# The last expert blocks of a stage return their results by a product with ones

## The chip, the cores and the metric

The kernel runs on one core of one Trainium2 chip. The metric is the device time of one execution in microseconds; before the change its median over three runs is 806.35 us (805.9 to 808.5).

## The reference, cut to what matters

Four batches of 256 tokens with 128 features go through four layers. Each layer adds a gated attention and a gated feed-forward to x. Two of the four feed-forwards route tokens to experts, and the change touches only these:

```python
# layer 1: one of 8 experts for each token
scores = feats @ centroids.T
expert = jnp.argmax(scores, axis=1)
onehot = jax.nn.one_hot(expert, E)
alpha = sigmoid(sum(feats * centroids[expert]))
ys = vmap(_sublayer, ...)(feats, gamma, beta, W1, b1, W2, b2)   # normed -> 128x512 -> relu -> 512x128
y = jnp.einsum('te,etd->td', onehot, ys)
out = alpha * y + (1.0 - alpha) * feats
# layer 3: two of 8 experts for each token, and a shared one
scores = softmax(xt @ gate_w.T)
topk_w, topk_i = jax.lax.top_k(scores, 2)
eo = einsum(silu(xt @ gate_k) * (xt @ up_k), down_k)            # for each expert
y = weighted sum of the two experts' eo;  shared = silu(xt @ sh_gate) * (xt @ sh_up) @ sh_down
# in the model
x = x + tanh(g_ffn[l]) * ffn_l(layernorm(x))
```

The reference computes every expert for every token. The kernel computes only the chosen ones.

## The kernel before, in words

**Groups and streams.** The batches are taken in two groups of two (G = 2), 512 tokens in a group, four tiles of 128 tokens. `chain(g)` writes one group's work in order: attention and feed-forward of layer 0, attention 1, `route1` and `feed1` (layer 1's experts), attention 2 and feed-forward 2, attention 3, `route3` and `feed3` (layer 3's experts). Each piece is a Python generator, a stream. A stream yields an estimate in us of what it has just written, and `run_streams` always continues the stream with the smallest sum. So the order of instructions on each engine is fixed when the kernel is built; the two groups and their pieces interleave by these estimates. On the chip each engine works its queue strictly in this order, and an instruction that waits holds up everything behind it on its engine. SP's queue issues most loads, ACT's queue some loads, the outputs and the writes of expert results, POOL's queue all indirect transfers.

**Slots and blocks.** `Routed.assign` counts the tokens of each expert and gives every choice of a token a slot (`si`, one number for each token tile and choice) in a list where each expert's slots begin at a multiple of 128. A block is 128 slots and has one expert. With 512 choices there are 11 blocks (layer 1), with 1024 there are 15 (layer 3); slots that no token holds carry zeros. `dispatch` (L744) scatters the tokens' rows to their slots in memory, one indirect transfer of 128 rows for each token tile and choice, from POOL; `empty_slots` (L662) has zeroed that memory from SP near the beginning. `fetch` (L770) reads four blocks of rows back with one transfer on SP.

**A stage's call.** `Routed.run` goes over the blocks. For block j: `ask` reads the expert's number into a register of SP and loads the down weights (L801), and starts the next fetch; `before` copies the up weights on DVE (L808) and transposes the block on PE (L810; the result is scaled or copied at L1109 or L1318 on DVE); `up` is the first product and its activation (L1115 to L1121, or L1324 and L1283, L1284); `down` is the second (L819, four matmuls, recorded as eight), its result is copied by ACT (L824) to a tile `ys` of four blocks, and each full `ys` is written to memory (`back`, L826). `down` of a block stands on PE behind `up` of the next.

**Results.** When all blocks are done, `run` gathers from `back` the row of each token's slot (L851): four indirect transfers in layer 1, eight in layer 3, on POOL. `feed1` adds them to the experts' bias, weighs them by alpha and adds the result to x (L1125 to L1131); `feed3` adds them to the shared expert's result with their weights (L1338), multiplies by the gate into x (L1344) and writes the output (L1348).

The steps that follow: after `feed1`, the next attention of that group begins with statistics of x (L270, L272 on DVE, L274 and L276 on POOL), query transposes (L1165), scores (L328), row maxima (L338); `finish2` normalises x again (`x2f`, L282). Tiles `feat`, 20 in rotation, hold most intermediate results, `ys` and the gathered rows among them.

Names in the profile: `x1n`, `x3f` are the rows that are scattered, `rows_f` the slots' memory, `xs_f` the fetched rows, `pt_f` and `xT_f` their transpose, `ph_f` or `pp_f` the first product, `h_f` its activation, `wd_f` the down weights, `py_f` the second product, `ys_f` its copy, `back_f` the results' memory, `yg_f` the gathered rows.

Of the kernel before, what the change touches and what calls it, by code (L numbers as in the profile page):

```python
# [18 lines left out]
P = 128  # L19
B, S, D = 4, 256, 128  # L20
T = S // P
G = 2
# [14 lines left out]
def flamingo_kernel(ctx: ExitStack, tc: tile.TileContext, a: dict, out: bass.AP):  # L37
# [619 lines left out]

    def empty_slots():
        for layer, k in ((1, 1), (3, 2)):
            for g in range(B // G):  # L660
                t = dram.tile([blocks(k) * BLOCK, D], F32, tag=f"rows{layer}", name=f"rows_f{layer}_{g}")
# [6 lines left out]
    class Routed:  # L668
# [7 lines left out]
        def assign(self, hots, src, after=()):  # L676
# [62 lines left out]
            yield from self.dispatch()  # L739

        def dispatch(self):

            for i, t, src in self.moves:
# [12 lines left out]
                yield 1.3  # L756

# [25 lines left out]
        def run(self, width, weights, down_weights, turn, up, cost):  # L783
# [4 lines left out]
            name, n = self.name, self.n  # L788
            back = dram.tile([n * BLOCK, D], F32, tag=f"back{len(self.slots)}", name=f"back_{name}")
            bv = back.rearrange("(j p) d -> p j d", p=P)  # L790
# [24 lines left out]
            def down(j, h):  # L815
# [9 lines left out]
                if j % 4 == 3 or j == n - 1:  # L825
                    nc.scalar.dma_start(out=bv[:, j // 4 * 4 : j + 1, :], in_=ys[0][:, 0 : j % 4 + 1, :])  # L826

# [7 lines left out]
            for j in range(n):  # L835
                st, xT = ready.pop(0)
                h = up(st, xT, f"{name}_{j}")
                if behind:
                    down(*behind)
                ask(j + 2)  # L840
                behind = (j, h)
                if j + 2 < n:
                    ready.append(before(j + 2))
                yield cost
            down(*behind)
            yield 4.0
            self.out = []
            for i, si in enumerate(self.slots):
                y = feat(f"yg_{name}_{i}").rearrange("p (t d) -> p t d", t=GT)
                for t in range(GT):  # L850
                    nc.gpsimd.indirect_dma_start(  # L851
                        y[:, t, :], None, back, bass.IndirectOffsetOnAxis(ap=si[:, t : t + 1], axis=0)
                    )
                self.out.append(y)
            yield 8.0
# [219 lines left out]
    def route1(g):  # L1075
# [22 lines left out]
        acc = work.tile([P, GT, D], F32, tag="acc", name=f"f1acc_{g}")  # L1098
        nc.vector.tensor_copy(acc, pb)
        groups1[g] = (r, fe, al, acc)  # L1100
        r.fetch(0)
        yield 4.0


    def feed1(g):
        r, fe, al, acc = groups1[g]
# [17 lines left out]
        yield from r.run(518, shared["we1"], a["L1f_down"], turn, up, 1.9)  # L1124
# [382 lines left out]
```

## Time and profile before

| what | us |
|---|---|
| median of three runs | 806.35 |
| the profiled execution | 805.46 |
| its span, first to last instruction | 803.7 |
| PE busy (matmuls) | 719.7 |
| DVE busy | 462.6 |
| ACT busy | 314.9 |
| POOL busy | 133.5 |
| the 24 gathers of results (L851), mean of one | 0.994 |
| the 24 scatters of rows (L744), all | 25.3 |

The profiled execution is the profiler's record of one run: its own time is 1.8 us more than its span. Engines are PE (matmuls; PEld are its weight loads), DVE, ACT, POOL and SP. Issuing a transfer is not counted as busy, except on POOL, where building an indirect transfer is an instruction of about 1 us. An entry in square brackets says how long the engine had been idle before the instruction and what ended that. The granted clock is that of PE, as a share of full speed; its mean over the execution is 0.958.

### The profile page before, as it was taken

Reading aid. Unit: us, or ns where it says so; the run is one execution under the profiler, and the core shown is the slowest. Engines: PE = TensorE matmul, PEld = TensorE weight load, DVE = VectorE, ACT = ScalarE, POOL = GpSimd, SP = SyncE. Lnnn points to the kernel's source line nnn. Section 1 sums busy time; section 2 is a strip of 40 time slices with the busy share of each in tenths; the row PEclk is TensorE's granted clock in tenths of the full one; section 3 lists DMA queues with packets and bytes.
Section 4 is the critical chain, followed back from the end, with each engine's and each line's share of the span. In section 5 each row is a group of like instructions: output and inputs, shape, how many; then the busy total and the mean of one; then the engine's idle time right before and its main releaser. Section 6 shows DMA issues by size and latency. Waiting matters only on the chain.

```text
span 803.7 us, 14819 instructions
## 1 busy us (share of the span) xinstructions
PE 719.7 (90%) x5756; PEld 515.6 (64%) x5756; DVE 462.6 (58%) x1179; ACT 314.9 (39%) x609; POOL 133.5 (17%) x233
## 2 busy tenths in 40 slices
PE   5989998999999998997897899979999988799990
PEld 4556676766666665597864456546666645599990
DVE  3475573556577587775767476553454436665461
ACT  2536555343444423232453445435542442322330
POOL 3010121321110001313212131010000004040043
PEclk9899999999999999999997899999999989999995
DMA  6820101101023002354471000000100200435631
GB/s 202 239 61 2 54 2 53 54 1 54 1 76 110 2 8 53 97 199 150 135 261 39 1 28 2 1 1 1 53 8 1 60 1 24 148 89 146 164 106 49
DMA packets 52986, 54.98 MB, mean 68 GB/s; under 512 B 7274, under 2 KB 40084, under 8 KB 52660
## 3 DMA queue, kind: packets, MB, share of 16 engines
q1 hardware_dynamic: 41252, 44.07, 18.5%
q10 hardware_dynamic: 10128, 6.82, 2.8%
q0 software_dynamic: 1536, 3.15, 1.3%
q8 instruction: 45, 0.74, 0.4%
q14 instruction: 25, 0.20, 0.1%
HBM read 44.52 MB, written 9.50 MB: 67 GB/s over the span
## 4 chain that ended last, share of the span: by engine, by line
PE 70%; DVE 15%; issue 6%; ACT 4%; POOL 2%; DMA 2%; DVEq 0%; POOLq 0%; ACTq 0%; SPq 0%
PE po_a L486 7%; PE sc_a L472 7%; PE pp_f L1324 6%; DVE nmx L338 4%; PE py_f L819 4%; PE po_a L374 4%; PE ps_a L501 4%; PE sc_a L328 4%; PE pf_a L559 3%; PE st_a L355 3%; PE pw_qh_a L444 3%; PE pv_a L458 3%; PE pw_kh_a L444 3%; PE f0pp L987 2%; PE pb_a L526 2%
## 5 line engine op out<-in xcount | busy, mean ns | idle before, releaser
L338 DVE TENSOR_REDUCE nmx<-sc_a 128x2 f32<-128x512 f32 x128 | 79.4, 683 | 27.1 <-PE sc_a L328 27.1
L366 ACT ACTIVATE pw_a<-st_a 128x512 f32<-128x512 f32 x128 | 66.1, 605 | 36.7 <-PE st_a L355 36.6
L472 PE MATMUL sc_a<-qh_a,kh_a 64*128 64x256 f32 x512 | 69.8, 402 | 0.6 <-DVE kh_a L72 0.4
L1042 ACT ACTIVATE pr_a<-pr_a 128x1024 f32<-128x1024 f32 x32 | 33.8, 1057 | 91.7 <-DVE pr_a L1041 85.4
L486 PE MATMUL po_a<-pr_a,va_a 128*64 128x256 f32 x512 | 63.3, 392 | 1.1 <-ACT va_a L76 0.6
L472 PEld LDWEIGHTS sc_a<-qh_a,kh_a 64*128 64x128 f32 x512 | 46.5, 190 | 23.1 <-issue 10.3
L1324 PE MATMUL pp_f<-xT_f,st_f 128*128 128x128 f32 x480 | 58.7, 276 | 1.9 <-DVE xT_f L1318 1.9
L819 PE MATMUL py_f<-wd_f,h_f 128*128 128x128 f32 x416 | 56.7, 279 | 1.7 <-DVE h_f L1121 1.7
L1324 PEld LDWEIGHTS pp_f<-xT_f,st_f 128*128 128x128 f32 x480 | 56.1, 192 | 3.3 <-issue 2.6
L819 PEld LDWEIGHTS py_f<-wd_f,h_f 128*128 128x128 f32 x416 | 51.8, 195 | 2.8 <-DVE h_f L1121 2.1
L486 PEld LDWEIGHTS po_a<-pr_a,va_a 128*64 128x64 f32 x512 | 35.2, 139 | 24.4 <-issue 5.6
L1215 DVE TENSOR_SCALAR pr_a<-pr_a 128x1024 f32<-128x1024 f32 x32 | 22.1, 691 | 47.7 <-ACT pr_a L1214 47.7
L1038 DVE SCALAR_TENSOR_TENSOR pr_a<-maskT,sc_a 128x512 f32<-128x512 uint8 x64 | 40.9, 680 | 11.7 <-PE sc_a L472 11.6
L1214 ACT ACTIVATE pr_a<-sc_a 128x512 f32<-128x512 f32 x64 | 34.0, 604 | 33.0 <-PE sc_a L472 33.0
L328 PE MATMUL sc_a<-kp,qp 32*128 32x256 f32 x512 | 44.2, 429 | 0.3 <-DVE lT L1223 0.3
L355 PE MATMUL st_a<-qm_a,kp 32*128 32x256 f32 x512 | 40.8, 428 | 2.4 <-DVE qm_a L348 2.4
L374 PE MATMUL po_a<-pw_a,va_a 128*32 128x256 f32 x512 | 42.5, 412 | 0.0
L494 ACT COPY oT_a<-po_a 128x512 f32<-128x512 f32 x32 | 18.6, 586 | 50.2 <-PE po_a L486 48.7
L355 PEld LDWEIGHTS st_a<-qm_a,kp 32*128 32x128 f32 x512 | 26.0, 200 | 17.7 <-DVE nmx L338 7.0
L1284 DVE TENSOR_TENSOR h_f<-pp_f,sl_f 128x512 f32<-128x512 f32 x30 | 20.6, 688 | 25.4 <-PE pp_f L1324 15.9
L851 POOL DMA_INDIRECT yg_f<-back_f,si_f x24 | 23.9, 994 | 67.8 <-DMA back_f<-ys_f 42.0
L991 POOL TENSOR_TENSOR wide<-f0wb,wide 128x512 f32<-128x512 f32 x16 | 20.3, 1270 | 88.9 <-DVE wide L990 80.4
(337 smaller groups left out, 1329.6 us busy)
## 6 DMA issues: line engine op xcount, KB each, us to landing
wd_f<-in_L3f_down_dram SPq DMA_DIRECT2D x30, 256.0 KB, 3.2
wd_f<-in_L1f_down_dram SPq DMA_DIRECT2D x22, 256.0 KB, 4.0
f0wb<-f0wd SPq DMA_DIRECT2D x32, 128.0 KB, 3.2
rb_a<-rw_a SPq DMA_DIRECT2D x16, 256.0 KB, 3.8
we<-in_L3f_experts_dram SPq DMA_DIRECT2D x8, 512.0 KB, 9.1
xs_f<-rows_f SPq DMA_DIRECT2D x10, 256.0 KB, 3.6
back_f<-ys_f ACTq DMA_DIRECT2D x10, 256.0 KB, 5.7
we<-in_L1f_experts_dram SPq DMA_DIRECT2D x8, 259.0 KB, 5.4
```

Source lines behind the costliest of these rows:

```text
L328: nc.tensor.matmul(self.sc[j][:, qt, :], lhsT=self.qp[c // 2][r, c % 2, qt * P : (qt + 1) * P], rhs=self.kp[c // 2][r, c % 2, :], start=Tr ...
L338: nc.vector.tensor_reduce(self.nmx[c % 2][:, :, j, 8], self.sc[j], AX.X, ALU.max, negate=True)
L355: nc.tensor.matmul(st[j][:, kt, :], lhsT=self.kp[c // 2][r, c % 2, kt * P : (kt + 1) * P], rhs=self.qm[c // 2][r, c % 2, :], start=True, s ...
L366: nc.scalar.activation(pw[:, i], st[2 * n + i], AF.Exp, scale=SCALE8)
L374: nc.tensor.matmul(po[r, :], lhsT=self.va[:, kt, 4 * c + j, :], rhs=pw[j // 2][:, j % 2, kt, :], start=(kt == 0), stop=(kt == T - 1),)
L444: nc.tensor.matmul(pp[:, ci, :], lhsT=w[:, c * P : (c + 1) * P], rhs=src, start=True, stop=True)
L472: nc.tensor.matmul(sc[jj][:, kt * S : (kt + 1) * S], lhsT=self.kh[c // 2][r, c % 2, kt * P : (kt + 1) * P], rhs=self.qh[c // 2][r, c % 2, ...
L486: nc.tensor.matmul(po[64 * jj : 64 * jj + 64, ci, :], lhsT=self.va[cp // 2][:, kt, 4 * (cp % 2) + 2 * ci + jj, :], rhs=self.prs[2 * cp + c ...
L819: nc.tensor.matmul(py, lhsT=h[:, f, :], rhs=wd[:, f * P : (f + 1) * P], start=(f == 0), stop=(f == 3))
L1038: nc.vector.scalar_tensor_tensor(pr[:, jj, :], maskT[:, b].rearrange("p t q -> p (t q)"), -1e32, sc[jj], ALU.mult, ALU.add)
L1214: nc.scalar.activation(pr[:, jj, :], sc[jj], AF.Exp)
L1324: nc.tensor.matmul(pp[i][:, f * P : (f + 1) * P], lhsT=st[:, 512 * i + f * P : 512 * i + (f + 1) * P], rhs=xT, start=True, stop=True,)
```

## The change

A table names three of the four calls and how many of their last blocks are concerned: the last 3 of 11 in layer 1, both groups, and the last 4 of 15 in layer 3's second group. Layer 3's first group has none.

- For these calls, `empty_slots` also zeroes the last blocks of `back` and a small list `tags`, one number (layer 1) or two (layer 3) for each slot.
- After `dispatch`, a new stream `label` scatters to each slot its token's number in the group (from 1) and, in layer 3, its weight: four indirect transfers on POOL in layer 1, eight in layer 3. Then SP reads the last blocks' tags to a tile, and that read waits for all of these scatters.
- `belongs` makes on DVE, for each of the last blocks, a matrix of 128 slots by 512 tokens that is one (or the weight) where the slot is the token's; a count of 1 to 512 for this comes from POOL.
- `sent_back` multiplies this matrix with the block's results in `ys` on PE: four matmuls, one for each token tile. All last blocks add up in one tile of PSUM, `pb_f`.
- The last blocks are not written to `back`. The gathers form a stream of their own, which begins when the other blocks have been written; rows of slots in the last blocks read as zero. Their adds on DVE stand in that stream.
- Bias, alpha and gate are now applied piece by piece and everything is added to x directly: features and bias in `route1`, the shared expert in `shared3`, gathered rows and the product as they come. The tile `acc` and the final multiplies are gone. In layer 3 the output of a batch is issued after the last add to it.

The diff, cut to its core:

```diff
+    LAST = {"f1_0": 3, "f1_1": 3, "f3_1": 4}
+    results_of = {}
     def empty_slots():
...
+                if last:
+                    nc.sync.dma_start(out=bv[:, n - last :, :], in_=zero.unsqueeze(1).to_broadcast([P, last, D]))
+                    tags = dram.tile([n * BLOCK, k], F32, tag=f"tags{layer}", name=f"tags_f{layer}_{g}")
+                    cleared = nc.sync.dma_start(
+                        out=tags.rearrange("(p j) k -> p (j k)", p=P), in_=zero[:, 0 : n * k]
+                    )
...
             yield from self.dispatch()
+            self.last = LAST.get(name, 0)
+            if self.last:
+                self.labelled = Stream(self.label(weights))
...
+        def label(self, weights):
+            tags, cleared = results_of[self.name][2]
+            k, last = len(self.slots), self.last
+            src = small.tile([P, k, GT, k], F32, tag=f"tag{k}", name=f"tag_{self.name}", bufs=1)
+            nc.gpsimd.iota(src[:, :, :, 0], pattern=[[0, k], [P, GT]], base=1, channel_multiplier=1, ...)
+            if weights:
+                for i, w in enumerate(weights):
+                    nc.gpsimd.tensor_copy(src[:, i, :, 1], w)
+            yield 1.0
+            writes = []
+            for i, si in enumerate(self.slots):
+                for t in range(GT):
+                    write = nc.gpsimd.indirect_dma_start(
+                        tags, bass.IndirectOffsetOnAxis(ap=si[:, t : t + 1], axis=0), src[:, i, t, :], None
+                    )
...
+                    nc.gpsimd.memset(spare, 0.0)
+                    yield 1.3
+            self.tags = small.tile([P, last, k], F32, tag=f"tags{k}", name=f"tags_{self.name}", bufs=1)
+            read = nc.sync.dma_start(
+                out=self.tags, in_=tags.rearrange("(j p) k -> p j k", p=P)[:, self.n - last :, :]
+            )
+            for w in writes:
+                self.need(read, w)
...
-                if j % 4 == 3 or j == n - 1:
+                if j >= n - last:
+                    back_to.append((j, ys[0][:, j % 4, :]))
+                elif j % 4 == 3 or j == n - 1 - last:
                     nc.scalar.dma_start(out=bv[:, j // 4 * 4 : j + 1, :], in_=ys[0][:, 0 : j % 4 + 1, :])
+                    if j == n - 1 - last:
+                        back_to.append(Stream(gathered(), 4.0))
+            def gathered():
+                out = []
+                for i, si in enumerate(self.slots):
+                    y = feat(f"yg_{name}_{i}").rearrange("p (t d) -> p t d", t=GT)
+                    for t in range(GT):
+                        nc.gpsimd.indirect_dma_start(
+                            y[:, t, :], None, back, bass.IndirectOffsetOnAxis(ap=si[:, t : t + 1], axis=0)
+                        )
+                        yield 1.3
+                    out.append(y)
+                yield 1.5
+                for i, y in enumerate(out):
+                    for t in range(GT):
+                        add(i, t, y[:, t, :])
+                        yield 0.5
+            def belongs(j):
+                if "count" not in once:
+                    once["count"] = feat(f"count_{name}")
+                    nc.gpsimd.iota(once["count"], pattern=[[1, GN]], base=1, channel_multiplier=0, ...)
+                m = feat(f"m_{name}_{j}")
+                tag = self.tags[:, j - (n - last), :]
+                if len(self.slots) == 2:
+                    nc.vector.tensor_scalar(m, once["count"], tag[:, 0:1], tag[:, 1:2], ALU.is_equal, ALU.mult)
+                else:
+                    nc.vector.tensor_scalar(m, once["count"], tag[:, 0:1], None, ALU.is_equal)
+                return m
+            def sent_back(j, y):
+                if "sums" not in once:
+                    once["sums"] = ps_mm([P, GT, D], f"pb_{name}")
+                for t in range(GT):
+                    nc.tensor.matmul(once["sums"][:, t, :], lhsT=ms[j][:, t * P : (t + 1) * P], rhs=y,
+                                     start=(j == n - last and t == 0), stop=(j == n - 1 and t == GT - 1))
...
             for j in range(n):
                 st, xT = ready.pop(0)
                 h = up(st, xT, f"{name}_{j}")
+                if len(back_to) > 1:
+                    sent_back(*back_to.pop())
                 if behind:
                     down(*behind)
+                if j == n - 1 - last and last:
+                    yield from joined(self.labelled)
+                if j >= n - last:
+                    ms[j] = belongs(j)
                 ask(j + 2)
...
+            if len(back_to) > 1:
+                sent_back(*back_to.pop())
             down(*behind)
-            yield 4.0
...
-            yield 8.0
+            yield HOP
+            if last:
+                sent_back(*back_to.pop())
+            yield from joined(*back_to)
+            if last:
+                for t in range(GT):
+                    add(None, t, once["sums"][:, t, :])
...
     def feed1(g):
+        def add(i, t, y):
+            xt = x[G * g + t // T][:, t % T, :]
+            nc.vector.scalar_tensor_tensor(xt, y, al[:, t : t + 1], xt, ALU.mult, ALU.add)
...
     def feed3(g):
+        def add(i, t, y):
+            b, xt = G * g + t // T, x[G * g + t // T][:, t % T, :]
+            w = tg[:, 7:8] if i is None else weight[i][:, t : t + 1]
+            nc.vector.scalar_tensor_tensor(xt, y, w, xt, ALU.mult, ALU.add)
+            if t % T == T - 1 and i == ending:
+                nc.scalar.dma_start(out=out[b].rearrange("(t p) d -> p t d", p=P), in_=x[b])
+        ending = None if r.last else 1
```

## The prediction

> **What bounds the kernel now.** I read the page's chain first, then the end of the timeline by engine, then the stretch where the first expert stage of both groups meets the next attention.
>
> The chain that ended last, by engine:
>
> ```profile
> ## 4 chain that ended last, share of the span: by engine, by line
> PE 70%; DVE 15%; issue 6%; ACT 4%; POOL 2%; DMA 2%; DVEq 0%; POOLq 0%; ACTq 0%; SPq 0%
> ```
>
> PE bounds most of the span, so what delays PE's queue in the middle costs its whole length. The end is different. Timeline of the last 20 us (start, us, engine, line):
>
> ```profile
> 784.62 0.27 ACT L824 COPY ys_f<-py_f 128x128 f32<-128x128 f32 x1 [0.87 <-PE py_f L819]
> 784.92 0.37 ACTq L826 DMA_DIRECT2D back_f<-ys_f  x1
> 787.79 0.94 POOL L851 DMA_INDIRECT yg_f<-back_f,si_f  x1 [13.52 <-issue]
> ...
> 796.52 0.94 POOL L851 DMA_INDIRECT yg_f<-back_f,si_f  x1 [0.30 <-issue]
> ...
> 799.08 0.35 DVE L1338 SCALAR_TENSOR_TENSOR f3acc<-yg_f,f3m,f3acc 128x128 f32<-128x128 f32 x1 [0.83 <-DMA yg_f<-back_f,si_f]
> 799.35 0.87 DVE L1344 SCALAR_TENSOR_TENSOR x<-f3acc,tg,x 128x256 f32<-128x256 f32 x2
> ```
>
> PE is done at 784.6. Then come the write to memory, eight gathers 1.25 us apart, their adds and the output, to 803.7: 19 us with nothing beside them. In the middle, PE, POOL and SP:
>
> ```profile
> 372.68 1.15 PE L1097 MATMUL f1pb<-b2r,f1hT 8*128 8x128 f32 x8
> 376.73 0.44 PE L810 MATMUL pt_f<-ident,xs_f 128*128 128x128 f32 x2 [2.90 <-DMA xs_f<-rows_f]
> 377.56 2.07 PE L1115 MATMUL ph_f<-xT_f,st_f 128*128 128x128 f32 x8 [0.39 <-DVE xT_f L1109]
> ...
> 383.87 0.27 PE L810 MATMUL pt_f<-ident,xs_f 128*128 128x128 f32 x1
> ...
> 398.94 1.15 PE L328 MATMUL sc_a<-kp,qp 32*128 32x256 f32 x16
> ...
> 426.71 1.15 PE L328 MATMUL sc_a<-kp,qp 32*128 32x256 f32 x16
> ...
> 438.28 0.66 PE L294 MATMUL pt_x<-ident,x2f 128*128 128x128 f32 x2 [0.96 <-DVE x2f L282]
> ```
>
> ```profile
> 370.69 0.96 POOL L744 DMA_INDIRECT rows_f<-x1n,si_f  x1 [0.21 <-issue]
> 371.65 0.09 POOL L755 MEMSET spare<- 1x8 f32 x1
> 377.76 1.13 POOL L851 DMA_INDIRECT yg_f<-back_f,si_f  x1 [6.02 <-PE pt_f L810]
> ```
>
> ```profile
> 376.72 0.42 SPq L770 DMA_DIRECT2D xs_f<-rows_f  x1
> ```
>
> At 383.87 PE transposes block 4 of group 1, whose rows SP had fetched at 376.72. POOL has 6 us free after the four dispatches, and PE idles 2.90.
>
> **The last stage (gain 9.0).** Blocks 11 to 14 of the last call no longer go through memory; the gathers need only blocks 0 to 10.
> - Gathers: block 10's product ends at 775.2 and its write can issue at 775.55. From write to first gather it took 787.79 - 784.92 = 2.87, so gathers start at 778.4, the eighth issues 7 x 1.25 later at 787.15 and lands 2.46 later (796.52 to 798.99 in the chain) at 789.6.
> - Products: one is four 128x128 matmuls, like a down product (0.89 from start to start in the chain). Those of blocks 11, 12 and 13 stand ahead of the last down product: 2.7. That of block 13 waits for ACT's copy just before it: 0.5. On ACT the outputs of group 0 now stand ahead of the gate of block 12 and wait for six adds in a row on DVE (0.30 apart), so the last up product starts about 0.45 late. The last copy moves from 784.62 to 788.2; copy 0.4 and product 0.9 give 789.5.
> - Both sides meet at 789.6. Then one add (0.35) and four adds of the sums (0.30 each) end at 791.2. Before, the last arithmetic ended at 800.22 and the span at 803.7, 3.5 later. So 794.7: 9.0 saved. Removed with it are the two L1344 multiplies. Group 0's last call keeps all its gathers; its adds go straight into x, in idle time of DVE.
> - Bounds: the trace's times to landing of the write are 4.3 / 5.7 / 7.1 (least, median, most), but none is that of a lone last write. With 5.7, gathers start at 781.25 and 6.1 is saved; with gathers never last, the products give 9.5. I take 9.0, from the write nearest in place, when no weights load.
> - Masks (four) and the count: a 128x1024 tensor-scalar takes 0.69, a 128x512 one from PSUM 0.68, so 0.35 to 0.68 each; they lie in DVE's 1.3 us of idle time per block. If that were gone, xT of the next block would be late by as much.
>
> **The f3_1 labels (0).** Eight scatters of 1.27 on POOL, from 721.7 to about 732. POOL's next work is a gather at 763.7. SP's read of the tags stands behind the weights of group 0's last block, long after. Zeroing back and tags on SP follows 31.4, and SP is next needed at 88.9: 0. Cover for both is POOL's and SP's idle time; a later scatter would cost only beyond 30 us.
>
> **The first expert stage, group 0 (0, at most +1).** Four scatters on POOL; the third and fourth stand behind a statistics step that ends at 341.9, so the last issues at 343.2 and lands 2.2 later (370.69 dispatch to the 373.07 fetch). SP's tag read waits for it, and behind it the weights of block 2 and the rows of blocks 4 to 7, which land at 351.1; PE asks at 351.5. Nearly no cover: each us later is a us on PE. DVE gains 2.5 us of adds into x, less 0.6 of copy, beside 3.0 of idle between the four L533 multiplies.
>
> **Where the two groups meet (+2.8).**
> - POOL: the count (an iota; 0.19 for 128x32, memset of twice its elements 0.95: 0.2 to 1.0, take 0.7) stands after the first dispatch of group 1. Then gathers of group 0 alternate with label scatters: four of each at 1.25 to 1.27 from 372.65 on, the last scatter at 381.7, landed at 383.9.
> - SP: the tag read waits for that, behind it the weights of block 2 and the rows of blocks 4 to 7. Read 0.4, register and weights 1.7, rows at 386.1, 3.6 to land: 389.7. PE asked at 383.87. Hold: 5.8. On DVE, the adds of gathers 1 to 4 stand between the steps of blocks 0 and 1, the last waiting until 383; this, the 2.7 us of products on PE and the wait for the count on DVE lie inside the hold.
> - Credit: x is complete earlier, and the order puts the attention's first steps ahead of blocks 5 to 7. After 389.7 come two up and two down products, the two query transposes, one more of each pair: 4.7 us; with slow matmuls about 2 us more (two lots of eight at 2.07 instead of 1.06), so the first scores start at 396.4 instead of 398.94.
> - From there to the second batch's scores: 27.8 us as before, plus three blocks (1.9 each) and three products (0.89): 8.4, less what PE's idle time and slow value products there (4.3) take in, half: 2.1. So 430.5 instead of 426.71: +3.8.
> - DVE's nine adds ahead of x2f (434.47 to 437.79) become eight, only four of them (1.2 us) between the maxima and x2f: the 0.96 wait at 438.28 goes. +2.8.
> - Later PE's order is the same and it is busy 91 to 95% up to 660, so I carry the whole. Bounds: nothing slow and all idle filled gives -1.4; slow matmuls for twice as long and nothing filled gives +6.9.
>
> On the slow matmuls, the row: after 2.90 of idle, eight matmuls took 2.07 instead of 1.06, and the granted clock was 0.81 from 377 to 395. The Trainium skill, "TensorE: Matmul & The Clock Gate", Part 1, says that about 3.4 us without work halves the clock and 3.4 us of sustained work restore it. By that rule the hold costs some 1.7 us beyond its length, an estimate, against my 2.
>
> On the tags, the row: 512-byte rows land 2.2 us after issue; no row shows smaller scatters. The Trainium skill, "DMA: Bandwidth & Descriptors", Specifications, says that transfers under 512 B are done by read-modify-write; it gives no price, and it speaks against this change.
>
> **Sum.** The profiled execution took 805.46 (span 803.7). -9.0 + 2.8 = -6.2: **799.3 us**. It lies 0.9 below the median of the runs, 806.35, and as low as their lowest, 805.9, nearly.
>
> **Rivals.**
> - The hold is absorbed: the attention's early start and idle time pay for it. For it: 10 us of waits and slow matmuls from 373 to 427. Against: the rows land 5.8 late whatever PE does. -9.0 and -1.4 to +1: 795 to 797.5.
> - The middle at its upper bound and the write at its median: -6.1 + 6.9, or one of them with more: 803 to 806, no change that can be told.
> - Slower: SP held by the tag read. Each us that the last label lands after 383.9 is a us on PE at block 4. From 8.6 us late (landing at 392.5) the kernel is over 2.4 us slower; 11 late gives 810. For it: the 4-byte scatter has no row, and gathers and scatters share one queue. Against: the dearest gather in the trace lands in 4.0, and a label moves 4 bytes where a row moves 512.
>
> **How the numbers follow.** Forecast 0.48 (797.5 to 803), absorbed 0.25, no change 0.13, slower 0.14. This measurement can tell about 0.3%, 2.4 us, from no change: faster 0.73, same 0.13, slower 0.14. Range 794.8 to 806: it leaves out the slower case and little below.
>
> **What would show it.** The end: PE done near 789, last gather issued near 787, the span's end some 7 us after the last down product instead of 19. The middle: PE waiting at the transpose of block 4 until about 390 for the fetch of rows, POOL busy from 372 to 383, the first scores at 396, the second batch's at 430. I am wrong if scatters of tags land much later than 2.2 us, if the last gathers wait for the write, or if PE makes up the hold before 480.

## The result, and the profile after

The changed kernel is slower. Its median is 818.91 us (813.45 to 825.24, four runs) against 806.7 (805.9 to 808.5) for the kernel before on the same chip: 1.0148 times the time, 95% interval 1.0101 to 1.0196, some 12 us. The profiled execution took 813.45, the fastest of its runs, with a span of 811.7 (before: 805.46 and 803.7), so the two traces account for 8.0 of it. Medians here and below are of all runs of a kernel, and ratios leave out the few runs that fell into a slower state.

The chain of the changed kernel by engine, and ahead of it the busy times:

```profile
PE 731.3 (90%) x5836; PEld 530.2 (65%) x5836; DVE 467.9 (58%) x1207; ACT 314.0 (39%) x607; POOL 156.5 (19%) x273
```

```profile
## 4 chain that ended last, share of the span: by engine, by line
PE 33%; DVE 8%; POOL 3%; DMA 2%; issue 2%; ACT 2%; POOLq 0%; DVEq 0%; SPq 0%; ACTq 0%
```

PE is still the largest part. The shares add up to half of the span, so the chain was followed back only that far, and its 33% is not to be set against the 70% of before. POOL is busy 23 us more, with 16 labels among the rest, and PE 11.6.

The end of the timeline of the changed kernel (start, us, engine, line), beside the lines that the prediction showed of before:

```profile
792.38 0.37 ACTq L876 DMA_DIRECT2D back_f<-ys_f  x1
...
795.25 0.98 POOL L887 DMA_INDIRECT yg_f<-back_f,si_f  x1 [2.83 <-DVE x L1435]
...
802.78 1.16 PE L918 MATMUL pb_f<-ys_f,m_f 128*128 128x128 f32 x8 [0.35 <-ACT ys_f L872]
```

Block 10's write is issued at 792.38, the first gather 2.87 later, and PE works on beside the gathers. From this write to the end of the span it is 19.3 us; the prediction had 19.15 (775.55 to 794.7). In the trace of before ACT's copy of block 10 starts at 775.23, so this write could have gone at 775.53. Here it goes 16.8 us later and the end comes only 8.0 later: the last stage saved 8.8. So in this trace the change does at the end what it was forecast to do, and what went wrong lies before it.

The labels (L790) by tile, in the changed kernel, with the time from issue to landing in the last line:

```profile
L790 POOL DMA_INDIRECT tags_f<-tag_f,si_f x16: 964/1030/1312, 333.5 to 745.8; - x16
DMA to landing us min/median/max: 3.8/5.5/8.2
```

The prediction took 2.2, the landing of a 512-byte row. First place where it shows: block 4 of group 0's first expert stage, on PE, POOL and SP.

```profile
347.44 1.06 PE L867 MATMUL py_f<-wd_f,h_f 128*128 128x128 f32 x8
351.80 0.33 PE L858 MATMUL pt_f<-ident,xs_f 128*128 128x128 f32 x1 [3.30 <-DMA xs_f<-rows_f]
```

```profile
341.04 1.29 POOL L790 DMA_INDIRECT tags_f<-tag_f,si_f  x1
```

```profile
345.79 0.38 SPq L800 DMA_DIRECT2D tags_f<-tags_f  x1
346.68 0.33 SPq L849 DMA_DIRECT2D wd_f<-in_L1f_down_dram  x1
347.11 0.38 SPq L818 DMA_DIRECT2D xs_f<-rows_f  x1
```

The last label is issued by 342.3, SP's read of the tags can start only at 345.79, behind it come weights and the rows of blocks 4 to 7, and PE stands 3.30 us. PE had come to this block some 3 us sooner than before (its last down product ahead of the block starts at 347.44, before at 350.62); after the wait it is 0.29 later than before (351.80 against 351.51), so the labels eat a lead here. Second place, where the groups meet, on POOL, SP, DVE and PE:

```profile
375.48 0.98 POOL L887 DMA_INDIRECT yg_f<-back_f,si_f  x1 [0.21 <-issue]
...
382.23 0.98 POOL L790 DMA_INDIRECT tags_f<-tag_f,si_f  x1 [0.30 <-issue]
```

```profile
388.72 0.38 SPq L800 DMA_DIRECT2D tags_f<-tags_f  x1
```

```profile
385.67 0.35 DVE L1224 SCALAR_TENSOR_TENSOR x<-yg_f,f1al,x 128x128 f32<-128x128 f32 x1 [4.74 <-DMA yg_f<-back_f,si_f]
...
388.70 0.41 DVE L1227 TENSOR_SCALAR xT_f<-pt_f,st_f 128x128 f32<-128x128 f32 x1
```

```profile
389.16 2.07 PE L1233 MATMUL ph_f<-xT_f,st_f 128*128 128x128 f32 x8 [5.89 <-DVE xT_f L1227]
...
400.40 1.15 PE L328 MATMUL sc_a<-kp,qp 32*128 32x256 f32 x16
...
435.21 1.15 PE L328 MATMUL sc_a<-kp,qp 32*128 32x256 f32 x16
```

SP's read starts 5.5 us after the last label's issue has ended. PE stands 5.89, as long as predicted, yet at the second block and not the fifth: POOL's queue holds labels between the gathers, and the gather of 375.48 landed 10.2 us after its start (385.67). The add that waits for it stands on DVE ahead of the second block's transposed copy, and PE waits for that. Before, gathers (L851) landed in 4.0 at most. Third place, the labels of the last call:

```profile
742.61 0.52 PE L858 MATMUL pt_f<-ident,xs_f 128*128 128x128 f32 x2 [3.28 <-DMA xs_f<-rows_f]
```

PE stands 3.28 for the rows of the next blocks while eight labels are on their way (735.9 to 746.8). In the trace of before nothing waits for rows at this place.

### The profile page after: what moved, and what is told of

Read it like the earlier page. It is cut to its first block, busy times and chain, and to the rows that moved or that the text cites. A ratio compares the mean times of both kernels' runs of the same rounds, so it can differ in the third digit from the quotient of the medians.

```text
span 811.7 us, 15053 instructions
## 1 busy us (share of the span) xinstructions
PE 731.3 (90%) x5836; PEld 530.2 (65%) x5836; DVE 467.9 (58%) x1207; ACT 314.0 (39%) x607; POOL 156.5 (19%) x273
## 4 chain that ended last, share of the span: by engine, by line
PE 33%; DVE 8%; POOL 3%; DMA 2%; issue 2%; ACT 2%; POOLq 0%; DVEq 0%; SPq 0%; ACTq 0%
PE pp_f L1448 5%; PE po_a L486 4%; PE sc_a L472 4%; DVE nmx L338 3%; PE py_f L867 2%; PE ps_a L501 2%; PE pw_qh_a L444 2%; PE pv_a L458 2%; PE po_a L374 2%; PE pw_kh_a L444 1%; PE pf_a L559 1%; PE sc_a L328 1%; PE st_a L355 1%; POOL yg_f L887 1%; PE pb_a L526 1%
## 5 line engine op out<-in xcount | busy, mean ns | idle before, releaser
L1448 PE MATMUL pp_f<-xT_f,st_f 128*128 128x128 f32 x480 | 62.8, 288 | 2.3 <-DVE xT_f L1442 2.3
L1448 PEld LDWEIGHTS pp_f<-xT_f,st_f 128*128 128x128 f32 x480 | 60.0, 203 | 3.9 <-DVE xT_f L1442 2.3
L1145 DVE SCALAR_TENSOR_TENSOR pr_a<-maskT,sc_a 128x512 f32<-128x512 uint8 x64 | 40.9, 681 | 11.7 <-PE sc_a L472 11.6
L374 PE MATMUL po_a<-pw_a,va_a 128*32 128x256 f32 x512 | 38.8, 405 | 0.0
L1398 DVE TENSOR_TENSOR h_f<-pp_f,sl_f 128x512 f32<-128x512 f32 x30 | 20.6, 687 | 27.0 <-PE pp_f L1448 19.4
L1233 PE MATMUL ph_f<-xT_f,st_f 128*128 128x128 f32 x176 | 27.4, 305 | 8.9 <-DVE xT_f L1227 8.9
```

Of the source, the lines that this page charges most:

```text
L374: nc.tensor.matmul(po[r, :], lhsT=self.va[:, kt, 4 * c + j, :], rhs=pw[j // 2][:, j % 2, kt, :], start=(kt == 0), stop=(kt == T - 1),)
L1145: nc.vector.scalar_tensor_tensor(pr[:, jj, :], maskT[:, b].rearrange("p t q -> p (t q)"), -1e32, sc[jj], ALU.mult, ALU.add)
L1448: nc.tensor.matmul(pp[i][:, f * P : (f + 1) * P], lhsT=st[:, 512 * i + f * P : 512 * i + (f + 1) * P], rhs=xT, start=True, stop=True,)
```

## The experiments

Each of the five groups ran on another chip. The kernel before took 815.58, 819.2 and 816.71 us in the first three, 805.95 and 807.19 in the last two, like the 806.7 of the first comparison. Ratios are always to it on the same chip, with the 95% interval.

### Which call, and is it the size of the labels?

Labels of 512 bytes instead of 4 or 8, the values the same:

```diff
-  tags = dram.tile([n * BLOCK, k], F32, ...)
+  tags = dram.tile([n * BLOCK, D], F32, ...)
-  src = small.tile([P, k, GT, k], F32, ...)
+  src = small.tile([P, 2, GT, D], F32, ...)[:, 0:k]
-  in_=tags.rearrange(...)[:, self.n - last :, :]
+  in_=tags.rearrange(...)[:, self.n - last :, 0:k]
```

> The changed kernel with labels of 512 bytes instead of 4 or 8: each scatter writes a whole row of 128 equal labels (f3_1: its weight in the second column), and the read takes only the first columns. Number, order and place of the scatters, the read, the masks and the products stay. Theory S (small label writes hold up every transfer beside them): labels land in 2.2 to 2.8 us after issue instead of 3.8 to 8.2, the gathers beside them in 2.5 to 4 instead of up to 10.2, the hold of 5.89 us on PE at block 2 of f1_1 falls below 2, the hold of 3.28 us on f3_1's first rows below 1, and the time comes to 800 to 808. Theory Q (what costs is that gathers and labels alternate in one queue and that SP's read waits for the last label, whatever their size): landings fall by less than 1 us, both holds stay, 812 to 820.

819.8: 1.0063 [1.0024, 1.0102]. In its trace the wait at block 4 of group 0's first expert stage is gone: that transpose starts at 354.91 with no idle time before it. Where the groups meet PE still stands, in a wait that ends in nothing the profile names, and beside layer 3's labels two down products are 9.3 us apart, where 2.8 to 6.8 are usual:

```profile
387.03 2.08 PE L1234 MATMUL ph_f<-xT_f,st_f 128*128 128x128 f32 x8 [3.71 <-issue]
```

The change for layer 3's second group alone, for layer 1 alone, and the first of these with a longer estimate ahead of the labels:

```diff
-    LAST = {"f1_0": 3, "f1_1": 3, "f3_1": 4}
+    LAST = {"f3_1": 4}                  # second kernel: {"f1_0": 3, "f1_1": 3}
+                yield 12.0              # third kernel only, ahead of the labels
```

> Products only in the last stage: LAST holds f3_1 alone; both first expert stages send everything through memory, in the new form of the code. If the last stage gives what its steps say, the end comes 8.75 us earlier against the write of block 10, less the hold of 3.3 on f3_1's first rows: 806.5 - 8.75 + 3.3 = 801, range 799 to 803.5, with runs as close together as those of the kernel before. If the loss is in the last stage or in the order of the whole program, and not in the first expert stages: 808 or more. If the spread of the changed kernel's runs (813 to 825) comes from labels beside gathers, it is gone here.

> Products only in the two first expert stages: LAST holds f1_0 and f1_1. If the loss is there: the delay of PE at the second batch's scores is 8.5 us as in the changed kernel, some of it made up later, and the last stage gives nothing back: 811 to 820, with the wide spread of the changed kernel. If the first stages' delay is made up before the last stage (rival of an absorbed hold): 805 to 808.

> As the kernel with products in the last stage only, and its eight label scatters are put 12 us later in the order, behind the fetch of f3_1's first rows. If the labels beside this fetch make the 3.28 us hold: the hold is gone or below 0.5 and the time is 2.5 to 3.5 below that kernel, about 798. If the hold comes from the rows' own landing (3.95 us after the last dispatch) and not from labels: no difference between the two.

816.35: 0.9991 [0.9948, 1.0033]; 827.44: 1.0161 [1.0107, 1.0216]; 812.85: 0.9971 [0.9937, 1.0005]. Layer 1 alone loses as much as the whole change did in the first comparison. Layer 3 alone gains nothing on this chip. Its labels cost it something (two down products beside them are 9.3 us apart), and its end saves less than in the first comparison: from block 10's write to the end of the span it takes 23.9 us, against 19.3 there and 28.2 for the same stretch in the kernel before. In between PE, ACT and DVE stand still beside the gathers, DVE for longest:

```profile
792.01 0.37 ACTq L876 DMA_DIRECT2D back_f<-ys_f  x1
...
806.37 0.69 DVE L1398 TENSOR_TENSOR h_f<-pp_f,sl_f 128x512 f32<-128x512 f32 x1 [7.53 <-remote]
```

In the traces from chips of this slower kind, an end with layer 3's part takes 22.6 to 26.0 us from that write, and in those from the others 19.0 to 19.4. The third kernel failed as an experiment: nothing else stands on POOL there, so the longer estimate left the labels at 721.6 to 731, where they had been, and its time says nothing of labels against fetches.

A second chip: 512-byte labels with layer 3 alone; labels of layer 1 as a 129th column of the rows, which the dispatch scatters anyway (layer 3 with 512-byte labels); the changed kernel and the kernel before once more.

```diff
-  t = dram.tile([blocks(k) * BLOCK, D], F32, ...)
+  w = D + 2 - k                                   # k = 1 in layer 1: 129 columns
+  t = dram.tile([n * BLOCK, w], F32, ...)
+  nc.gpsimd.iota(o[:, :, D], pattern=[[P, T]], base=label, channel_multiplier=1, ...)
+  read = nc.sync.dma_start(out=self.tags, in_=self.rv[:, self.n - self.last :, D : D + 1])
```

> Products in the last stage only, and its eight label scatters write 512 bytes each instead of 8. With 8 bytes the stretch of the scatters cost 10 to 13 us against the kernel before (matmuls of one block came in pieces of 9, 2, 1, 2, 1, 1, and handshakes between engines took 2 to 4 us). Theory S (small label writes slow everything beside them): that stretch costs at most 3 us, and the ratio to before is 0.986 to 0.992. Rival I (any indirect transfer on POOL beside working engines slows them, whatever its size): the stretch stays long, the ratio is 0.996 to 1.000, as with 8 bytes.

> As the changed kernel, with 512-byte labels in f3_1, and in the first expert stages no label scatters at all: each row carries its token's number as a 129th column (rows of 516 bytes), and SP reads this column for the last three blocks. If the label scatters and the waits for them are what the first stages lose: the hold of 3.3 us at block 4 of f1_0 and the hold of 5.9 us in f1_1 are gone or below 2, and the time is within 0.3% of the kernel with products in the last stage only. If it is the products, masks and gathers themselves (PE's three products of 1.06 in each call, DVE's adds between the blocks): a loss of 5 us or more stays against that kernel.

> The changed kernel again, beside the others on one chip: ratio to before 1.010 to 1.020 if the first comparison (1.0148) holds here too.

> The kernel before, for its trace on this chip. If late handshakes come with every indirect transfer beside work on other engines (rival I), its row dispatch of f3_1 and its gathers show them too: blocks on PE longer than 2.79 us while POOL issues. If they come with small writes alone (theory S): blocks of 2.79 us throughout, as in the first trace.

Layer 3 alone with 512-byte labels 816.59: 0.9943 [0.9909, 0.9977]; riding in layer 1 825.34: 1.0056 [1.002, 1.0091]; the changed kernel 840.39: 1.0259 [1.0235, 1.0283]; the kernel before, one run, 816.53. So the changed kernel is 1.5% slower on one chip and 2.6% on another, and with 512-byte labels 0.6% on a third. That points to the size, across chips only; the fourth group settles it on one chip, and for layer 3's eight scatters alone. For layer 1's four-byte labels among the gathers no run here tells size from number. The whole change with 512-byte or riding labels is still no faster than before; layer 3 alone with 512-byte labels is, by 0.6%. The two kernels of this group with 512-byte labels in layer 3 differ by layer 1's part, whose labels ride and need no scatter: it costs 1.1%, some 9 us, all the same.

On these chips there is a second loss, which the traces of the first comparison do not show. The changed kernel of this group beside layer 3's labels, ACT and then PE:

```profile
736.49 0.27 ACT L872 COPY ys_f<-py_f 128x128 f32<-128x128 f32 x1 [6.71 <-remote]
747.13 0.60 ACT L1397 ACTIVATE sl_f<-pp_f 128x512 f32<-128x512 f32 x1 [10.38 <-issue]
```

```profile
742.88 0.56 PE L1448 MATMUL pp_f<-xT_f,st_f 128*128 128x128 f32 x1 [0.34 <-issue]
744.99 0.37 PE L1448 MATMUL pp_f<-xT_f,st_f 128*128 128x128 f32 x1 [1.54 <-issue]
```

POOL issues its eight labels from 736.93 to 746.82, and ACT's next activation comes 0.3 after the last; PE issues the matmuls of one product singly, with pauses that end in nothing that the profile knows. Two down products, 2.8 apart elsewhere, are 17.1 apart there. With 512-byte labels (the first kernel of this group) it was still 16.1. So this second loss stands beside a run of indirect transfers on POOL, whatever their size. The kernel before shows it here too, in a smaller form. Beside its row scatters two down products are 4.5 apart (723.30 and 727.75), and beside the gathers of group 0 they are 6.0 and 4.5 apart:

```profile
780.65 1.26 PE L819 MATMUL py_f<-wd_f,h_f 128*128 128x128 f32 x8 [3.09 <-DVE h_f L1284]
```

These two stretches hold 7 of the 11.1 us by which this span (814.8) exceeds that of before in the first comparison (803.7). That the transfers cause the standstill is argued from where it stands; no run shows how.

### What do the labels cost altogether?

The changed kernel without the scatters of labels: the list stays zero, so no result of a last block reaches its token, while every product, mask and wait on the cleared list stays; the same with layer 3 alone; and layer 3 alone with rows of 130 columns, in which token and weight ride. The kernels without scatters also lose the other work of the labels on POOL, the numbering, the copies of the weights and the memsets between scatters.

```diff
-            for i, si in enumerate(self.slots): ...       # the scatters
+            writes = [cleared]
+            for _ in range(k * GT):
+                yield 1.3
```

```diff
+                w = D + 2 if last else D
+                nc.scalar.copy(x2[i][:, :, 0 : D + 1], xs[i][:, :, 0 : D + 1])
+                nc.scalar.copy(xs[i][:, :, D + 1], m[:, i * T : (i + 1) * T])
+                nc.scalar.copy(x2[i][:, :, D + 1], m2[:, i * T : (i + 1) * T])
+            src = [lambda t: xs[t // T][:, t % T, :], lambda t: x2[t // T][:, t % T, :]]
+                if j == 6 and last:
+                    self.ridden()                         # SP reads columns D and D + 1
```

> The changed kernel without its sixteen label scatters: the labels read are the zeros that were written at the start, so the masks are all zero and the results of the last blocks of the three calls do not reach their tokens. Reads, masks, products, gathers and the order of all else stay. If the scatters make the loss (they hold up the transfers beside them, and on the second chip the engines too): 12 to 20 us less than the changed kernel on the same chip, ratio to before 0.992 to 1.003. If products, masks and moved gathers make it: within 4 us of the changed kernel.

> Products in the last stage only, and no label scatters (the labels read are zeros, so the results of the last four blocks of f3_1 do not reach their tokens). This is what the last stage gains when its labels cost nothing. By my step 1 (8.75 us against the write of block 10 in the changed kernel's trace): ratio 0.987 to 0.991. If the engines are late in the tail beside the eight gathers in any case (products end 4 to 8 us late there in the runs on the second chip): 0.994 to 0.998.

> Products in the last stage only, with labels that ride: the rows that f3_1 dispatches are 130 wide, and their last two columns carry token and weight (a second copy of the rows for the second choice), so there is no scatter more than in the kernel before. Should equal the kernel without labels within 2 us, with the whole result: 0.988 to 0.994, the fastest of all kernels here. If the gain of the run without labels came from leaving out work and not from the scatters: as with 512-byte labels, 0.994 or more.

> The changed kernel beside these on one chip, as their reference: ratio to before between 1.010 and 1.030.

Without labels 815.21: 0.9998 [0.9953, 1.0044]; layer 3 alone without labels 807.51: 0.9896 [0.9854, 0.9938]; riding 807.99: 0.9926 [0.9889, 0.9963]; the changed kernel 833.11: 1.0212 [1.0156, 1.0269]. The label scatters, with their work on POOL, cost 2.1%, 17 us. Layer 3 alone without labels gains 1.0%, 8 us, and layer 1's part costs that much again. Even without labels the end is not clean on this chip: beside the last gathers ACT stood 5.89 us, and from block 10's write it takes 26.0 us, so that only about 2 of the 8 us come from there in this trace.

The rest has another source, which the name "layer 3 alone" hides. All these kernels carry the new form of the sums in layer 1 too: bias, features and gathered rows are added to x as they come, and the nine adds that stood in a row on DVE before (385.72 to 389.0) are gone. The traces show what that does. From the `f1pw` products of group 1 in layer 1 to the first scores:

```profile
367.92 1.04 PE L1198 MATMUL f1pw<-ident,hot_f 128*8 128x128 f32 x8
...
391.78 1.15 PE L328 MATMUL sc_a<-kp,qp 32*128 32x256 f32 x16 [0.43 <-ACT kp L1269]
```

These lines are of layer 3 alone on a chip of the first kind; before, the two stand at 370.63 and 398.94. It is 28.2 to 28.4 us in four traces whose layer 1 is that of before and 23.8 to 25.0 in eight traces with layer 3 alone, on both kinds of chips. From the same start to the first value product of attention 3, near 520, it is 154.1 to 155.4 against 147.2 to 149.4, some 6 us less; about 4 of them are left by layer 3's shared product, near 707. No run has the new form and nothing else, so its share of the time is read from these traces and not measured.

### Size or number?

Back on a chip of the first kind. The labels of layer 3 alone, spread out by memsets on POOL between them; the kernel before with eight scatters that nobody reads, put behind the row scatters of layer 3's second group, of 512 bytes and of 8 bytes; and layer 3 alone as it is.

```diff
+                    for _ in range(3):                    # first kernel, ahead of each label
+                        nc.gpsimd.memset(pause, 0.0)      # pause: 128 x 1024
```

```diff
+            for i, t, src in self.moves:                  # second and third: width 128 or 2
+                write = nc.gpsimd.indirect_dma_start(
+                    other, bass.IndirectOffsetOnAxis(ap=self.slots[i][:, t : t + 1], axis=0), src(t)[:, 0:width], None
+                )
```

> Products in the last stage only, with 8-byte labels as in the kernel that has this and no more, but three memsets of 128x1024 on POOL (about 2.9 us) ahead of each label scatter, so that the scatters come about 4 us apart and not 1.3. If what stalls the other engines is a long unbroken run of indirect transfers on POOL (rows and labels together 16 in 21 us): the stall is gone or below 3 us, ratio 0.988 to 0.995. If each small write costs by itself (1 to 2 us of late work for each): the sum stays, 0.997 or more.

> The kernel before, and behind f3_1's eight row scatters eight more of the same 512-byte rows into a tensor that nobody reads. No work is added on any other engine, and nothing waits for them. If any indirect transfers in a long run stall the engines: 4 to 10 us slower, ratio 1.004 to 1.012. If only small writes do: 0.998 to 1.002.

> The same with eight scatters of the first 8 bytes of each row. If size matters beside the length of the run: slower than the one with 512 bytes by 3 to 8 us, ratio 1.008 to 1.02. If only the run's length counts: equal to it within 2 us.

> Products in the last stage only, with unspaced 8-byte labels, on the same chip as the spaced one: 0.997 to 1.002 as before.

Eight scatters of 512 bytes: 805.95, 1.0006 [0.998, 1.0032]. The same eight with 8 bytes: 810.3, 1.0048 [1.0021, 1.0076]. Their landing, by tile, first 512 bytes, then 8:

```profile
DMA to landing us min/median/max: 2.3/3.7/4.9
```

```profile
DMA to landing us min/median/max: 2.7/4.4/6.9
```

And what PE sees with 8 bytes, at the transposes of the fetched rows:

```profile
731.13 1.06 PE L836 MATMUL py_f<-wd_f,h_f 128*128 128x128 f32 x8
732.02 0.27 PE L827 MATMUL pt_f<-ident,xs_f 128*128 128x128 f32 x1
734.69 0.41 PE L827 MATMUL pt_f<-ident,xs_f 128*128 128x128 f32 x2 [2.39 <-DMA xs_f<-rows_f]
735.46 3.52 PE L1341 MATMUL pp_f<-xT_f,st_f 128*128 128x128 f32 x16 [0.37 <-DVE xT_f L1335]
...
740.85 1.06 PE L836 MATMUL py_f<-wd_f,h_f 128*128 128x128 f32 x8
```

Down products 9.7 apart here are 6.8 apart before and with 512 bytes. So with the number and the place the same, the size alone costs 3.9 us by the ratio and 4.4 by the medians, and the trace shows 2.9 in this one place.

Layer 3 alone, unspaced: 799.43, 0.9923 [0.9895, 0.995]. That is near the 9.0 that the prediction gave to this part, less its labels (its two down products were 9.5 apart there, 2.7 too many). The agreement is partly chance, for the new form of layer 1 stands in this time too. Spaced: 807.25, 1.0016 [0.9991, 1.0041], worse by 7.8. Spaced labels landed in 2.4 / 2.9 / 5.0, nearly like rows, but the last came at 758 and the read of the tags and the weights behind it were late: PE waited 1.34 us for down weights and 1.70 for rows between 765 and 768. The test meant to tell whether the standstill of ACT and PE comes from the length of POOL's run, but it fell on a chip without the standstill, so that stays open.

### The two versions that were left

Layer 3 alone with riding token and weight (its result is the whole one), and the changed kernel without label scatters, both as above, on a chip of the first kind.

> Products in the last stage only, labels riding in rows of 520 bytes. On a chip where the kernel before takes about 806 us: the 2.7 us that 8-byte labels cost f3_1's first rows there are gone, ratio 0.987 to 0.991 against 0.9923 with scattered labels. On a chip where it takes 815 or more: 0.989 to 0.996 as before.

> The changed kernel without label scatters (the results of the last blocks of the three calls do not reach their tokens). Beside the riding kernel it gives what masks and products cost in the first expert stages: six products of 1.06 on PE and what they push. If PE pays for them in full there: 5 to 9 us above the riding kernel (ratio 0.995 to 1.001). If they are hidden on the prompt chip: within 2 us of it.

797.49 (790.97 to 802.04): 0.9858 [0.9822, 0.9894], the fastest, 1.4% under the kernel before. Without labels 802.54: 0.9939 [0.9907, 0.9972]. The latter's trace answers most of what follows. Its PE at the two places of layer 1 and at the scores:

```profile
348.55 0.27 PE L842 MATMUL pt_f<-ident,xs_f 128*128 128x128 f32 x1
...
381.61 1.09 PE L851 MATMUL py_f<-wd_f,h_f 128*128 128x128 f32 x8
...
390.01 1.15 PE L328 MATMUL sc_a<-kp,qp 32*128 32x256 f32 x16
...
424.82 1.15 PE L328 MATMUL sc_a<-kp,qp 32*128 32x256 f32 x16
```

With labels the same instructions start at 351.80, 391.03, 400.40 and 435.21: 3.25, 9.4, 10.4 and 10.4 later. Both holds are gone with the labels, and the spans are 801.4 and 811.7.

## Why the prediction was wrong

It said 799.3, faster with a chance of 0.73; its slower rival had 0.14. The step that failed stands in three of its terms: that a label scatter lands like a 512-byte row, in 2.2 us, and holds up nothing else. Labels landed in 3.8 to 8.2, median 5.5, and a gather and fetches of rows beside them came late: PE stood 3.30, 5.89 and 3.28 us at three places. By the medians with and without label scatters they cost some 17 us, where the forecast had the hold of 5.8.

**The last stage (-9.0): right on chips of the first kind.** 8.8 in the trace. Eight gathers were issued in 9.27 from first to last, against 8.75. With layer 3 alone the kernel ended 0.8% (with labels) and 1.4% (riding) under the kernel before, on such chips, part of it by the new form of layer 1. On the slower chips the end took 22.6 to 26.0 us from block 10's write instead of 19, so only 2 to 6 were saved there.

**The f3_1 labels (0): failed.** I named POOL's and SP's idle time as cover and did not ask who else uses the DMA queues in that stretch. The fetch of rows does, and PE waits for it: 3.28 us in the changed kernel, 2.7 with layer 3 alone, 3.9 as the price of eight 8-byte scatters in the kernel before. On the slower chips the standstill comes on top, and its cause stays open.

**Group 0's first expert stage (0 to +1): right against before, by luck of two errors.** The last label was issued 2.2 us sooner than forecast (341.04 instead of 343.2) and took about 2.5 longer to land; the rows came 0.29 later than PE had asked in the old trace. But PE now asked 3 us sooner, which I had not seen, and that lead was lost to the labels: without them this instruction starts at 348.55.

**Where the groups meet (+2.8): failed by its place.** The rival had SP held by the tag read, and I had the hold at block 4, with the products of group 0 (2.7) lying inside it. The tag read did start late, at 388.72 where I had about 384. But PE was stopped sooner, at the second block: DVE stood at an add whose gather was 10.2 us under way between small writes. I had taken these adds as done "until 383", from gathers in a trace that has no small writes in it. So the products came ahead of the hold and were not covered: the delay of PE goes from 0.29 at group 0's block 4 to 2.8 at 379.57 (the products) and to 9.95 at 391.03 (the hold of 5.89 and its slow matmuls), where I had 5.8 for all of it. What follows went as forecast: the credit up to the first scores is 8.45 (9.95 to 1.5; I had 5.8 to -2.5, 8.3), and from first to second scores it is 34.8 us against my 34.1. First scores at 400.40 instead of 396.4, second ones at 435.21 instead of 430.5.

**Layer 1 without its labels.** Take the hold away and my account of layer 1 would be 2.8 - 5.8 = -3.0. The trace without labels is 2.2 us ahead of that of before at 519, near this. The medians are less kind: without labels 0.9939 is -4.9 us, and with 8.8 from the last stage layer 1 costs 3.9, where I had -3.0. Against layer 3 alone, with no label scatters of layer 1 on either side, it costs 0.8% on one chip (0.9939 and 0.9858), 1.0% on another (0.9998 and 0.9896) and 1.1% on a third (1.0056 and 0.9943), 6.5 to 9 us. The first figure is the smallest, and the new form of the sums, which layer 3 alone has too, is a likely reason: part of what I had counted as the credit of layer 1's change comes without its products. Six products of about 1.1 us on PE, the bound here, would be 6.4 of the cost; that this is the cause was not shown by a run of its own.

**The sum.** -6.2 was forecast and +8.0 is in the traces, 14.2 apart. At 519 us the delay is +5.1 where +2.8 was forecast (2.3). Between 519 and 701 the changed kernel's trace loses another 8.3 against that of before, through longer half-clock stretches. Then come 3.3 at the labels of layer 3, and 0.2 less is saved at the end: 2.3 + 8.3 + 3.3 + 0.2 = 14.1, nearly all of it. Most of the 8.3 need not be the change's: three other traces of the kernel before, one plain and two whose extra scatters come only after 701, lose 5.8, 4.1 and 6.1 over the same stretch against the first. Two traces alone would have put this down to the change. The medians with and without labels, 1.0148 and 0.9939 (from two chips of the first kind; on one of the slower 1.0212 and 0.9998), are the better account. By them the miss is 18.1, some 12 slower where 6.2 faster was forecast: the labels cost about 17 instead of the hold's 5.8, and layer 1 without them 3.9 instead of -3.0. The two traces show 10.3 of the labels' 17; the changed kernel's is that of its fastest run, 5.5 under its median.

**The rule that I cited.** The Trainium skill, "DMA: Bandwidth & Descriptors", Specifications, has read-modify-write below 512 B. The runs agree in direction: 0.48% for eight scatters of 8 bytes, 0.06%, which is no change that can be told, for eight of 512. No run shows the mechanism itself. I quoted it as speaking against this change and then priced the labels by the nearest row, which was of 512 bytes. Even the rows had a higher bound, the dearest gather's 4.0 for each label, and I took the least.

## What to carry to other kernels

Price small scattered writes by a run before trusting them: one kernel with eight extra scatters that nobody reads tells more than any row of larger ones, and the cost falls on whoever shares the queues at that time. If an index must go along with a row that is scattered anyway, put it into that row as one more column (for layer 3 alone 0.9858 riding against 0.9923 with labels of its own, on two chips of the first kind). Returning results by a product with ones pays where PE would stand idle, behind the gathers at the very end; in the middle, where PE is the bound, layer 1's part cost 6.5 to 9 us here even without its labels. A change that is cut down to one of its parts should also be looked through for what it still carries along: the new form of the sums in layer 1 had no run of its own.

## What the runs showed of the hardware

- Eight-byte labels of layer 3 landed in 2.8 / 4.8 / 6.6 us when issued 1.3 apart, and in 2.4 / 2.9 / 5.0 when issued about 4 apart, on one chip; other traffic beside them differed too, so the spacing may not be the whole reason. A gather between four-byte labels took 10.2 to land. Gathers took at most 4.0 in the kernel before and up to 6.1, median 3.2, in the changed kernel without labels.
- In the first three groups, while POOL issued a long run of indirect transfers, ACT and PE stood still without any wait that the profile names, and went on when the run ended (10.38 us of ACT's time in one place). Labels of 8 and of 512 bytes, gathers and row scatters all had it beside them, in the kernel before too (3.09 us of PE's time beside gathers). The other two groups do not show it. Its cause was not found.
- The half clock can last several us at one place, and in two traces it lasted differently after much the same pause. From 540 to 548 the changed kernel's PE was busy without a pause and was granted half:

```profile
540.00:544.00 4.00, 4.00 (x14) 1.91 (x14) 1.59 (x4) 0.50 (x2) 0.21 (x1) 0.50 0.00 0
544.00:548.00 4.00, 4.00 (x11) 2.87 (x11) 1.18 (x2) 0.95 (x2) 0.00 (x0) 0.50 0.02 4
548.00:553.00 5.00, 5.00 (x18) 3.76 (x18) 0.87 (x2) 1.18 (x2) 0.00 (x0) 0.64 0.00 0
```

These are busy times of PE, its weight loads, DVE, ACT and POOL with their counts, then the granted clock and the DMA's share. The half clock lasted 13.6 us in all, for 12.8 of which PE worked (from 538.84); after the same pause the first trace of before had 3.4. The Trainium skill, "TensorE: Matmul & The Clock Gate", Part 1, has 3.4 us of sustained work as enough to restore the clock; the trace of before agrees, and here it took nearly four times that. What decides it is not settled. Nor is it why the kernel before takes 806 us on some chips and 815 to 819 on others.
